# Query, key and value projections of an attention block as seven block products each, with the element-wise work spread anew over three engines

## The chip, the cores and the metric

The kernel runs on one core of a Trainium2 chip. A core has a matrix engine (TensorE, PE in the profile, with its weight loads as PEld), a vector engine (VectorE, DVE), a scalar engine (ScalarE, ACT), a general engine (GpSimd, POOL), and a queue that only issues transfers (SyncE, SP). Each engine takes its instructions in the order in which they were written, and waits for other engines by semaphores. Matrix products land in PSUM[...]; everything else lies in SBUF.

The metric is the time of one execution on the device in microseconds. Before the change it is 1538.98 us, the median of three runs (1535.9 to 1542.12).

## What is computed

Input x has 8 sequences of 1024 rows with 512 features. Cut to what matters, the reference is:

```python
def attention(x):                       # 16 heads of 32
    Q, K, V = split(x @ Wq.T + bq), split(x @ Wk.T + bk), split(x @ Wv.T + bv)
    scores = Q @ K.T / sqrt(32)
    scores = where(j > i, -inf, scores) - (i - j)     # causal, with linear decay
    return merge(softmax(scores) @ V) @ Wo.T + bo

def ffn(x):
    xh = x @ H                           # Hadamard matrix 512 x 512
    scale = max(abs(xh)) / 7             # per row
    xq = clip(round(xh / scale), -8, 7) * scale
    return xq @ ternary(weight).T

x = x + layernorm(attention(layernorm(x)))
x = x + layernorm(ffn(layernorm(x)))
```

## The kernel before

**Tiles.** Rows are worked on in 16 chunks of 512 (two to a sequence), each of four row tiles of 128. Features lie in four blocks of 128. Because of the decay, a query only needs keys of its own block of 128 rows and of the block before: `band()` computes that, and at its end a flag says whether the scores were small enough for this to be exact; otherwise `general()` is run as well. With the given inputs it is not.

**Per chunk.** `norm_in` loads a row tile (xc), normalises it (xn) and transposes it on TensorE into xnT, 128 features by 512 rows for each of four feature blocks. `project_k`, `project_q` and `project_v` (lines 149 to 165) each make one block of 128 x 512 of k, q or v: four matrix products of 128 x 128 by 128 x 512 that add up in one PSUM bank (`project`, line 146), emptied by ScalarE (lines 152, 157, 165). There are 12 such blocks a chunk. GpSimd squares k and q (line 294); from the squares a bound of the scores is made (`bound`, `shift`), which is the bias of the exponentials.

**Per unit.** A chunk has eight units, each four heads by half of the chunk's rows. `scores` does the products s (line 401) and four exponentials on ScalarE (line 414); `mask` cuts off the triangle on GpSimd (line 425); `add_keys` adds the two key blocks' exponentials into `both` on VectorE (line 439), for the sums of the softmax; `values` does the products with v and the sums (lines 454, 463); `divide` ends the unit on VectorE (lines 479 to 484).

**Per row tile.** `rest` is a generator whose `yield`s part it into steps: load xr (177); output projection o (146); y with its statistics (182); x1, and two levels of the Hadamard transform as sums and differences u and w, and the statistics of x1 (189 to 200); transposes of w, copied as wT (205, 207); h, the remaining transform by a 128 x 128 matrix (211); a correction of h's first column, maximum, scale, the rounding by adding a large number (qf, qi: 213 to 229); transposes of qi, copied as qiT (234, 236); f, the ternary product (146); y2 with statistics (241); the last sums and the store (248 to 250).

**What sets the order.** Nothing is scheduled automatically inside `band()`: each engine's queue follows the order of the calls. The main loop (lines 573 to 628) walks the units in pairs u = 0, 2, 4, 6. In a pair it mixes the scores of two units, the values of two, three projection blocks of the next chunk, one step sequence `norm` of the chunk after that, and the steps of two row tiles, `rest_b` (the older) and `rest_a`. The order in one pair, on TensorE, is: scores, values of the unit before, a projection block, transposes of qi, o, f, scores, a projection block, values, transposes of w, transposes of xn, a projection block, h. All PSUM results other than s and the values share one pool of three banks, so a result's bank is needed again three results later.

**Start and end.** Weights are loaded by transfers that ScalarE issues (`load_weights`), x by SP. The first chunk's projections run ahead of the main loop (lines 528 to 546), with the norms of the second chunk and the preparation of the ternary weight (`prepare`) among them. After the loop the last two row tiles run in step (lines 635 to 640).

## Time and profile before

| | |
|---|---|
| median of three runs | 1538.98 us (1535.9 to 1542.12) |
| the profiled execution | 1541.74 us, of which 1540.0 us from the first to the last instruction (the span) |
| mean granted clock of TensorE over the span | 0.976 of full speed |
| instructions | 26488 |
| projections of k, q, v on TensorE (512 product instructions each) | 239.8, 237.2 and 233.7 us of busy time |
| key sums on VectorE, `both` (128 instructions) | 156.9 us |
| mask on GpSimd (128) | 141.7 us |
| squares of k and q on GpSimd (64 each) | 81.9 and 73.2 us |
| exponentials on ScalarE (512) | 296.1 us |
| read from and written to HBM | 39.13 MB and 16.78 MB |

The page names a group of instructions by its line in the kernel, the engine, the operation, and the tiles written and read, then gives the number of instructions, their busy time in us and the mean of one in ns, and last the idle time of the engine just before them with what ended it. The chain of waits follows the program back from its last instruction, each time to what released it. The timeline lists instructions in the order of time; neighbours of one kind are merged. An answer by windows gives each engine's busy time in a stretch. Busy times of TensorE are modelled at their ends and overlap, so a chain's step is a better measure of what a group costs than the sum of its busy times.

### The profile page before, as it was taken

To read this page: it belongs to the slowest core of one execution; us is meant where nothing else is said; L and a number is where in the kernel's file an instruction comes from. 1 tells how busy PE (TensorE), PEld (TensorE's weight loads), DVE (VectorE), ACT (ScalarE), POOL (GpSimd) and SP (SyncE) were. 2 spreads that over 40 slices of the span, in tenths; PEclk is the share of its full clock that TensorE was granted. 3 is DMA by queue.
4 is the path that set the end of the run, shared out by engine and by line. 5 is a ranking of instruction groups with operands and counts; after the bars stand their busy time and mean duration, and the time that the engine had idled before them with its cause. 6 is when DMAs were issued, how large, how long until landed. Compare 5 with 4: busy or idle time off the path is not lost.

```text
span 1540.0 us, 26488 instructions
## 1 busy us (share of the span) xinstructions
PE 1467.9 (95%) x10428; PEld 774.2 (50%) x10428; DVE 1037.0 (67%) x2284; ACT 572.0 (37%) x961; POOL 755.8 (49%) x1118
## 2 busy tenths in 40 slices
PE   3799999999999999999999999999999999999884
PEld 2345555555555555555555555555555555554552
DVE  2145767776777767777777767776777767666685
ACT  1123434334433434343434334343433444343331
POOL 1223555545555464555545555554654555354443
PEclk9899999999999999999999999999999999999777
DMA  5010011011101101110111011011101110000010
GB/s 193 20 29 15 22 42 42 21 42 42 43 21 42 42 25 39 42 42 21 42 42 38 26 42 43 28 35 42 42 22 42 42 42 21 29 28 28 16 42 23
DMA packets 31766, 57.70 MB, mean 37 GB/s; under 512 B 4241, under 2 KB 4369, under 8 KB 31633
## 3 DMA queue, kind: packets, MB, share of 16 engines
q1 hardware_dynamic: 27648, 50.34, 9.7%
q10 hardware_dynamic: 3984, 5.58, 1.0%
q8 instruction: 84, 1.38, 0.4%
q14 instruction: 50, 0.40, 0.1%
HBM read 39.13 MB, written 16.78 MB: 36 GB/s over the span
## 4 chain that ended last, share of the span: by engine, by line
PE 93%; DVE 3%; POOL 1%; DMA 1%; ACT 1%; issue 1%; ACTq 0%; POOLq 0%; DVEq 0%
PE q_ps L146 15%; PE k_ps L146 15%; PE o_ps L146 15%; PE v_ps L146 15%; PE s L401 8%; PE av L454 8%; PE h_ps L211 4%; PE av L463 4%; PE f_ps L146 3%; PE wT_ps L205 2%; PE xnT_ps L138 2%; PE qiT_ps L234 1%; DMA wk_sb<-in_wkT 0%; PE m_ps L367 0%; DMA wv_sb<-in_wvT 0%
## 5 line engine op out<-in xcount | busy, mean ns | idle before, releaser
L414 ACT ACTIVATE pr<-s,bias 128x512 f32<-128x512 f32 (+1 forms) x512 | 296.1, 661 | 391.2 <-PE s L401 328.7
L425 POOL TENSOR_SCALAR_AFFINE_SELECT pr<-pr 128x1024 f32<-128x1024 f32 x128 | 141.7, 1107 | 253.9 <-ACT pr L414 253.7
L146 PE MATMUL k_ps<-xnT,wk_sb 128*128 128x512 f32 x512 | 239.8, 613 | 0.7 <-ACT xnT L526 0.7
L146 PE MATMUL q_ps<-xnT,wq_sb 128*128 128x512 f32 x512 | 237.2, 607 | 0.0
L146 PE MATMUL o_ps<-wo_sb,oT 128*128 128x512 f32 x512 | 234.5, 601 | 0.2
L146 PE MATMUL v_ps<-wv_sb,xnT 128*128 128x512 f32 x512 | 233.7, 600 | 0.1
L439 DVE TENSOR_TENSOR both<-pr 128x1024 f32<-128x1024 f32 (+1 forms) x128 | 156.9, 1226 | 49.6 <-POOL pr L425 25.0
L146 PEld LDWEIGHTS k_ps<-xnT,wk_sb 128*128 128x128 f32 x512 | 94.4, 194 | 110.8 <-issue 107.2
L146 PEld LDWEIGHTS q_ps<-xnT,wq_sb 128*128 128x128 f32 x512 | 93.3, 192 | 106.4 <-issue 104.2
L401 PE MATMUL s<-qT,kT 32*128 32x128 f32 (+1 forms) x2816 | 144.9, 333 | 0.0
L146 PEld LDWEIGHTS v_ps<-wv_sb,xnT 128*128 128x128 f32 x512 | 93.1, 192 | 99.8 <-issue 99.0
L146 PEld LDWEIGHTS o_ps<-wo_sb,oT 128*128 128x128 f32 x512 | 92.8, 191 | 95.5 <-issue 92.4
L115 POOL TENSOR_SCALAR rstd_a<-mv_a 128x1 f32<-128x1 f32 x64 | 14.3, 223 | 252.9 <-DVE mv_a L123 252.9
L401 PEld LDWEIGHTS s<-qT,kT 32*128 32x128 f32 x2816 | 116.9, 190 | 41.3 <-issue 31.3
L454 PE MATMUL av<-pr,v 128*32 128x128 f32 (+1 forms) x2816 | 134.9, 323 | 0.6 <-DVE h_ps L213 0.6
L294 POOL TENSOR_TENSOR sqk<-kT 128x512 bf16<-128x512 f32 x64 | 81.9, 1280 | 70.4 <-ACT kT L152 70.4
L454 PEld LDWEIGHTS av<-pr,v 128*32 128x32 f32 x2816 | 76.5, 112 | 78.1 <-POOL rstd_c L116 20.5
L182 DVE TENSOR_TENSOR y<-o_ps,bo 128x512 f32<-128x512 f32 x64 | 44.3, 692 | 93.9 <-PE o_ps L146 93.9
L152 ACT ACTIVATE kT<-k_ps,bk_sb 128x512 f32<-128x512 f32 x64 | 44.0, 688 | 160.7 <-PE k_ps L146 160.7
L134 DVE TENSOR_SCALAR xn<-xc,mv_n,rstd_n 128x512 f32<-128x512 f32 x60 | 32.8, 547 | 105.0 <-POOL rstd_n L116 105.0
L165 ACT COPY v<-v_ps 128x512 f32<-128x512 f32 x64 | 37.5, 586 | 160.0 <-PE v_ps L146 160.0
L213 DVE SCALAR_TENSOR_TENSOR h_ps<-mv_b,h_ps 128x1 f32<-128x1 f32 x64 | 10.5, 164 | 126.5 <-PE h_ps L211 126.5
(121 smaller groups left out, 2156.6 us busy)
## 6 DMA issues: line engine op xcount, KB each, us to landing
xr<-in_x SPq DMA_DIRECT2D x64, 256.0 KB, 3.0
out<-y SPq DMA_DIRECT2D x64, 256.0 KB, 2.0
xc<-in_x SPq DMA_DIRECT2D x60, 256.0 KB, 2.8
wk_sb<-in_wkT ACTq DMA_DIRECT2D x4, 256.0 KB, 5.7
x<-in_x SPq DMA_DIRECT2D x4, 256.0 KB, 5.4
wq_sb<-in_wqT ACTq DMA_DIRECT2D x4, 256.0 KB, 4.4
wf_sb<-in_wf ACTq DMA_DIRECT2D x4, 256.0 KB, 4.7
wv_sb<-in_wvT ACTq DMA_DIRECT2D x4, 256.0 KB, 5.3
```

The lines of the kernel that those rows point to most:

```text
L146: nc.tensor.matmul(ps, lhs(k), rhs(k), start=(k == 0), stop=(k == KD - 1))
L152: nc.scalar.activation(kT[:, o, :], ps, AF.Identity, bias=bk_sb[:, o : o + 1])
L165: nc.scalar.copy(v[:, t, :], ps)
L182: nc.vector.tensor_tensor(y, ps, bo2, ALU.add)
L211: nc.tensor.matmul(xh[:, k * P : (k + 1) * P], wT[:, k, :], had_sb, start=True, stop=True)
L294: nc.gpsimd.tensor_tensor(sq, src[:, o, :], src[:, o, :], ALU.mult)
L401: nc.tensor.matmul(s[:, hh, sc : sc + w], kc.kT[hsl, g, at * P : (at + 1) * P], ch.qT[hsl, g, q0 + qc : q0 + qc + w], start=True, stop=True,)
L414: nc.scalar.activation(pr[:, :, r0:, own, cols], s5[:, :, r0:, own, cols], AF.Exp, bias=ch.bias[:, own, h : h + 1],)
L425: nc.gpsimd.affine_select(out=own, in_=own, compare_op=ALU.is_ge, fill=0.0, base=0, pattern=[[0, HPG], [0, 2], [1, P]], channel_multiplier=-1,
L439: nc.vector.tensor_tensor(self.both[:, :, r0:], pr[:, :, r0:, 0, :], pr[:, :, r0:, 1, :], ALU.add)
L454: nc.tensor.matmul(av[hh * HD : (hh + 1) * HD, 0, qc : qc + w], kc.v[:, at, h * HD : (h + 1) * HD], pr[:, hh, sc : sc + w], start=(at_part ...
L463: nc.tensor.matmul(av[hh * HD : (hh + 1) * HD, 1, :], ones[:, :HD], self.both[:, hh].rearrange("p r c -> p (r c)"), start=True, stop=True, ...
```

## The change

**Seven products.** From the second chunk on, each of q, k and v is seen as a product of two matrices of 2 x 2 blocks, 256 wide, and made from seven block products in place of eight, after a scheme of sums and differences. The weights' combinations are made once (`Weight.combine`: three new tiles and two overwritten), those of x once per chunk on GpSimd (`Projections.combine`, four differences of 128 x 512). `product` does one block product: four matrix products with 256 columns (each runs as two passes), into one PSUM bank. What was one ScalarE copy per block becomes: product 1 is copied by ScalarE with the bias; the results of 2, 6, 7, 5, 4 and 3 are added on VectorE to a running sum or into the destination, product 5 twice. A pair of units takes five products (six in u = 6) instead of three blocks: two after the first scores, one after the second, two or three after the transposes of xn. The order of q and k is swapped.

**Other work moved.** xn: from VectorE to ScalarE, with a new GpSimd instruction for its bias (nmr). Key sums: from VectorE to GpSimd; the copy of the first units to ScalarE. Squares of k and q: from GpSimd to ScalarE, two instructions of 128 x 1024. The variance after h: no statistics of x1 and no correction of the first column any more; a Hadamard block with a zero first column (had0_sb), ScalarE's square with a sum (var), two GpSimd instructions. qf: from VectorE to ScalarE, in a step of its own, so that `rest` has 12 steps.

**Start and end.** wk and two biases are loaded by ScalarE's queue; wq, wf, wv, wo and the rest by SP's, behind the loads of x and xc, of which xc now has two buffers instead of three. The scale of q is put into wq by four ScalarE instructions. The norms of the second chunk are begun one projection ahead of their transposes. The last tiles are advanced by a written string of steps. Many row buffers go from two to one, k and v from three to two, for the room that the combinations take.

```diff
@@ norm_in @@
-        xn = pools.row.tile([P, D], F32, tag="xn", name=f"xn_{name}", bufs=2)
-        nc.vector.tensor_scalar(xn, xc, mv[:, 0:1], r, ALU.subtract, ALU.mult)
+        xn = pools.row.tile([P, D], F32, tag="xn", name=f"xn_{name}", bufs=1)
+        nmr = pools.small.tile([P, 1], F32, tag="nmr", name=f"nmr_{name}")
+        nc.gpsimd.tensor_scalar(nmr, mv[:, 0:1], r, -1.0, ALU.mult, ALU.mult)
+        nc.scalar.activation(xn, xc, AF.Identity, bias=nmr, scale=r)
@@ rest @@
-        mvb = stats(small, x1, f"b_{n}")
-        rb = rstd_of(small, mvb[:, 1:2], 1, f"rstd_b_{n}")
         yield
...
-        nc.vector.scalar_tensor_tensor(
-            xh[:, 0:1], mvb[:, 0:1], -math.sqrt(D), xh[:, 0:1], ALU.mult, ALU.add
-        )
+        nc.scalar.activation(sq, xh, AF.Square, accum_out=var)
+        rb = small.tile([P, 1], F32, tag="rstd1", name=f"rstd_b_{n}")
+        nc.gpsimd.tensor_scalar(rb, var, 1.0 / D, EPS, ALU.mult, ALU.add)
+        nc.gpsimd.tensor_tensor(rb, rb, neghalf[:, :1], ALU.pow)
+        yield
...
-        nc.vector.tensor_scalar(qf, xh, isc, ROUND, ALU.mult, ALU.add)
+        yield
+        nc.scalar.activation(qf, xh, AF.Identity, bias=round_col, scale=isc)
@@ squares @@
-            nc.gpsimd.tensor_tensor(sq, src[:, o, :], src[:, o, :], ALU.mult)
+            for o in range(0, KD, 2):
+                nc.scalar.activation(sq[:, o : o + 2, :], src[:, o : o + 2, :], AF.Square)
@@ Projections @@
+            ORDER = (1, 2, 6, 7, 5, 4, 3)
+            def combine(self, which):
+                if which == 0:
+                    nc.gpsimd.tensor_tensor(t[:, 0], b12, b11, ALU.subtract)
+                    nc.gpsimd.tensor_tensor(t[:, 1], b22, t[:, 0], ALU.subtract)
+                else:
+                    nc.gpsimd.tensor_tensor(t[:, 2], b22, b12, ALU.subtract)
+                    nc.gpsimd.tensor_tensor(t[:, 3], t[:, 1], b21, ALU.subtract)
+            def product(self):
+                for o in range(HB):
+                    osl = slice(o * P, (o + 1) * P)
+                    for i in range(HB):
+                        a, b = (x, w) if kind == 2 else (w, x)
+                        nc.tensor.matmul(
+                            ps[:, o, :], a[:, i, osl], b[:, i, :], start=(i == 0), stop=(i == HB - 1)
+                        )
...
+                elif which == 2:
+                    nc.vector.tensor_tensor(c11, ps, self.u, ALU.add)
+                elif which == 6:
+                    nc.vector.tensor_tensor(self.u, ps, self.u, ALU.add)
...
+                elif which == 5:
+                    nc.vector.tensor_tensor(c22, ps, self.u3, ALU.add)
+                    nc.vector.tensor_tensor(self.u, ps, self.u, ALU.add)
+                elif which == 4:
+                    nc.vector.tensor_tensor(c21, ps, self.u3, ALU.add)
+                else:
+                    nc.vector.tensor_tensor(c12, ps, self.u, ALU.add)
@@ Unit.add_keys @@
-                nc.vector.tensor_tensor(
+                nc.gpsimd.tensor_tensor(
                     self.both[:, :, r0:], pr[:, :, r0:, 0, :], pr[:, :, r0:, 1, :], ALU.add
                 )
@@ main loop, one pair @@
                 new.scores()
+                if proj and u == 0:
+                    proj.combine(0)
                 if unit:
                     unit.values()
                     unit.divide()
                 unit = new
+                steps(rest_a, 1)
                 unit.mask()
+                unit.add_keys()
+                if proj and u == 0:
+                    proj.combine(1)
+                products(proj, 1)
                 norm = next(norms_due)
                 steps(norm, 1)
-                unit.add_keys()
-                if proj:
-                    proj.project()
-                    proj.square()
+                products(proj, 1)
                 rest_b = rest_a
                 steps(rest_b, 1)
                 rest_a = next(rests_due) if at or u >= 4 else None
                 steps(rest_a, 1)
...
                 new = Unit(ch, before, u + 1)
                 new.scores()
-                    proj.project()
+                products(proj, 1)
                 steps(rest_b, 1)
                 new.mask()
                 steps(rest_a, 1)
-                if proj:
+                if proj and u == 2:
                     proj.square()
                 unit.values()
                 new.add_keys()
                 unit.divide()
                 unit = new
                 steps(rest_b, 1)
                 steps(rest_a, 1)
                 steps(norm, 1)
-                if proj:
-                    proj.project()
-                    proj.square()
-                steps(rest_a, 2)
+                products(proj, 1)
+                if proj and u == 2:
+                    proj.bound()
+                products(proj, 2 if u == 6 else 1)
+                steps(rest_a, 1)
+                if proj and u == 4:
+                    proj.square()
+                steps(rest_a, 1)
@@ after the loop @@
-        steps(rest_a, 1)
-        last = [next(rests_due), next(rests_due)]
-        for step in range(1, REST):
-            if step in (2, 3, 4):
-                steps(rest_a, 1)
-            for r in last:
-                next(r)
+        tails = {"r": rest_a, "a": next(rests_due), "b": next(rests_due)}
+        for which in "rrarbarabraabaabbabababbabb":
+            next(tails[which])
@@ load_weights @@
-        wq_sb = load_weight(wqT, "wq_sb")
+        wq_sb = load_weight(wqT, "wq_sb", nc.sync, wts)
-        wf_sb = load_weight(wf, "wf_sb", big, "pr")
-        wv_sb = load_weight(wvT, "wv_sb")
+        wf_sb = load_weight(wf, "wf_sb", nc.sync, big, "pr")
+        wv_sb = load_weight(wvT, "wv_sb", nc.sync, wts)
+    def prepare_q(wq_sb, bias=True):
+        for k in range(KD):
+            nc.scalar.mul(wq_sb[:, k, :], wq_sb[:, k, :], 1.0 / ROOT_HD)
```

## The prediction

> **What bounds the kernel now.** I read the page's engine shares and its chain first, then the chain and the timeline of one pair of units in mid-kernel, then the waits of TensorE and the last chunk, which has no projections.

> ```profile
> PE 1467.9 (95%) x10428; PEld 774.2 (50%) x10428; DVE 1037.0 (67%) x2284; ACT 572.0 (37%) x961; POOL 755.8 (49%) x1118
> PE 93%; DVE 3%; POOL 1%; DMA 1%; ACT 1%; issue 1%; ACTq 0%; POOLq 0%; DVEq 0%
> ```

> TensorE is busy 95% and is 93% of the chain. In the windows of 100 us that I took between 190 and 1390 it is busy 99.98 us of each: in mid-kernel it waits for nobody, so time falls only if its own work falls, and rises as soon as it must wait. One pair of units, from the chain (start, us, what):

> ```profile
> 709.27 0.89 PE h_ps L211 x8
> 710.16 1.09 PE s L401 x24
> 711.25 1.00 PE av L454 x24
> 712.25 0.43 PE av L463 x8
> 712.68 3.63 PE k_ps L146 x8
> 716.32 0.22 PE qiT_ps L234 x4
> 716.54 3.49 PE o_ps L146 x8
> 720.03 0.86 PE f_ps L146 x4
> 720.89 1.09 PE s L401 x24
> 721.98 3.63 PE k_ps L146 x8
> 725.61 1.01 PE av L454 x24
> 726.62 0.43 PE av L463 x8
> 727.05 0.59 PE wT_ps L205 x4
> 727.64 0.44 PE xnT_ps L138 x4
> 728.07 3.44 PE k_ps L146 x8
> 731.51 0.89 PE h_ps L211 x8
> ```

> A pair takes 732.40 - 710.16 = 22.24 us and holds three projection blocks. The reader is to see how much TensorE work lies ahead of each point where it needs another engine. The tightest is wT, which needs VectorE's w:

> ```profile
> 720.07 0.69 DVE L182 TENSOR_TENSOR y<-o_ps,bo 128x512 f32<-128x512 f32 x1 [1.85 <-PE o_ps L146]
> 721.62 0.73 DVE L241 SCALAR_TENSOR_TENSOR y<-f_ps,sc,wscale_row 128x512 f32<-128x512 f32 x1
> 725.11 0.42 DVE L198 TENSOR_TENSOR w<-u 128x256 f32<-128x256 f32 x1
> ```

> VectorE runs without a gap from the end of o (720.03) to the end of w (725.53): 5.5 us, of which y2 (L241), its statistics, x1, u and w are 3.91. TensorE comes to wT at 727.05: 1.5 us to spare. In the last chunk, without projections, the spare is gone:

> ```profile
> 1441.14 0.79 PE L205 MATMUL wT_ps<-ident,w 128*128 128x128 f32 x4 [1.93 <-DVE w L197]
> ```

> ```profile
> 1426.00:1432.00 6.00, 5.91 (x63) 4.01 (x63) 0.78 (x3) 2.42 (x4) 0.50 (x1) 0.50 0.01 3
> ```

> The second fence is a window of the last chunk (busy PE, PEld, DVE, ACT, POOL, then the granted clock): after TensorE stood 3.36 us (from 1422.7 to 1426.1) its clock is 0.50 for six microseconds.

> [...] of five idle times of 3.36 to 3.42 us (34.0, 47.7, 65.4, 72.9, 1422.7) four were followed by 0.50, for about 6.7 us each time it can be timed. [...] here the add L249 takes 1263 ns for 512, so I estimate 2.4 us for 1024. [...] here rstd_b's pow took 1.54 us beside the add at L439 and 0.57 for rstd_n.

> **The change part by part**, on one chunk of four pairs (u = 0, 2, 4, 6).

> TensorE's own work. A pass of 512 columns takes 3.44/8 = 430 ns, one of 128 columns (h) 0.89/8 = 111; on the line between, 256 columns cost 217. Twelve blocks of 3.44 = 41.3 us become 21 of 8 x 217 ns = 36.5: -4.8 per chunk, -72 over 15 chunks (the first keeps whole products). Weight loads (190 ns mean) still fit under 217; if they did not, +0.5 per chunk. TensorE's floor is then 20.6 us a pair, plus one product of 1.73 in u = 6.

> The sums on VectorE: seven of about 0.69 and one more for "5", 14 us a chunk, against 20 removed (8 key sums of 1.28, st_b, xn, qf, the fix of h). Its load falls, so by share nothing is lost. What counts is place. VectorE takes its queue in order, and in the changed order the queue reads: y (o), its statistics, the sum of the pair's third product, y2 (f), statistics, x1, u, w. On TensorE: o, f, scores, third product, values (1.44), wT. So the sum cannot begin before the third product ends, and w follows it by 0.69 + 0.04 + 3.91 = 4.65, with about 0.1 to hand over. TensorE has only the values to do meanwhile: it waits 4.75 - 1.44 = 3.3 us at wT. Before, ScalarE emptied that block and y2 did not wait. This holds in u = 0 (product 6 of q), u = 4 (4 of k) and u = 6 (7 of v); in u = 2 the third product is 1 of k, emptied by ScalarE, and only the shorter spare bites: 5.5 + 0.1 against 0.86 + 1.09 + 1.92 + 1.44 = 5.3, so 0.3. Behind the waiting sum stand all of y2, x1, u, w, the division and the next sums; wT on TensorE waits for them, and all of TensorE behind wT.

> The GpSimd queue. Key sums 2.4 each, +19 less what the short units save, combinations of x 4 x 1.26 = 5, squares of 1.21 x 8 gone: some 16 us a pair of 24, not its bound. But place again: xn now is ScalarE's and waits for nmr, which waits behind mask and key sum on GpSimd, and qiT's copy stands behind xn on ScalarE. From the end of h: exps end 3.65, mask 4.8, key sum 7.2, rstd and nmr 8.3, xn 9.2, copy 9.8; f is reached at 9.9. It just fits. In u = 0 the four combinations stand in that queue (two before mask, two before rstd; net 3.0): f waits 3.0, about 2.3 in chunks whose first units have half a key sum.

> ScalarE. Squares of k (two of about 1.1) stand between h's Square and the exps of u = 6: qf and qi come late, 0.75 at qiT and 0.8 more at f. In u = 2 the squares of q delay wT's copy, whose PSUM buffer the next product but one needs: 0.9 to 1.1. Elsewhere the new Square, qf, xn (about 0.7 to 0.8 each) lie beside TensorE's work: qi is ready at 4.9, wanted at 6.2.

> Sum of waits: u = 0 6.3, u = 2 1.4, u = 4 3.3, u = 6 4.85: 15.85, or 14.95 in the other kind of chunk; 15.4 x 13, 12.7 for the chunk without norms, 6.5 for the first, where most rests are missing: +219.

> The clock. Waits of about 3.0 to 3.3: 43 at wT, some 10 at f. Not quite the 3.36 of the trace, so I take six in ten to halve the clock, at 3.0 us lost each (half of 6.7, less what falls into the wait): +95. From below 0 [...], from above all of them, +160.

> Start. Before, ScalarE issues the loads until 20.45 and k starts at 24.2; then four waits of 3.4 for xn behind GpSimd's squares (34.0, 47.7, 65.4, 72.9), with a halved clock after most. After, ScalarE issues wk and two biases alone, xn's chain stands a block ahead of its transposes, the squares go to ScalarE. New: the third xc load waits for a buffer freed by xn of the first tile, and wq, wf, wv, wo queue behind it on SP, so wq lands about 30; its scaling holds ScalarE till 32, and q needs it about 34. Scores begin near 74 instead of 99: -25; bounds -10 and -30.

> End. In the last chunk qi now passes exps and a second engine, +1.5 a pair; the staggered last tiles, one key sum of 2.4 for one of 1.28, -3 in all: +3, bounds -8 and +12. Other moves (st_b, fix of h, both's copy) lie under TensorE either way.

> Total against the profiled 1540.0: 1540 - 72 + 219 + 95 - 25 + 3 = 1760. That run took 1541.74 with what lies around the span, 2.8 above the median of the three runs: 1757.

> **Rivals.**
> - The waits come, the clock stays: 1757 - 95 = 1662. For: no wait of 3.3 stands alone in this trace. Against: four of five at 3.4.
> - Half the waits are taken up elsewhere (a buffer or a sum that I placed too late), little clock: 1540 - 72 + 110 - 25 = 1553, up to 1600.
> - Faster: the waits at wT stay under 1.6 us. Place: VectorE's queue between y and w, where the sum would have to be done by the time that f's result comes. At three per chunk that is the 4.8 saved; below it the fewer products decide, and with no waits the time is 1540 - 72 - 25 - 3 = 1440. For: TensorE is 93% of the chain and every other engine has a third of its time free. Against: the third product ends 3 us after f, and no queue is overtaken.
> - The products are not fewer: excluded by the changed order, 21 blocks of 256 columns a chunk.

> **How the numbers follow.** Forecast 0.66, clock stays 0.16, half the waits 0.07, faster 0.11. The range 1630 to 1820 leaves out the faster case, the half case and a tail of the clock's upper bound. A change under 0.5% can't be told from none; hardly any case ends there: faster 0.10, same 0.01, slower 0.89.

> **What would show it.** In the changed profile: TensorE busy under 90%, wT waiting for w about 45 times by about 3.3 us, f for the copy of qiT once a chunk; granted clock near 0.9; chunks of about 107 us instead of 90; passes of 256 columns at 217 ns; scores starting before 80. A wT wait near zero, or chunks under 90 us, would prove me wrong.

## The result, and the profile after

The changed kernel takes 1753.11 us (median of four runs, 1751.9 to 1754.21), the kernel before 1538.56 us in the four runs made with it: 1.1393 times as long, with a 95% interval of 1.1367 to 1.1418. The forecast was 1757. The profiled execution took 1754.21 us, with a span of 1752.5.

Of the page of the changed kernel, the engine shares, the chain by engine, and two groups of instructions:

```profile
PE 1488.5 (85%) x11508; PEld 1024.8 (58%) x11508; DVE 978.3 (56%) x2159; ACT 698.6 (40%) x1208; POOL 925.3 (53%) x1252
...
PE 47%; POOL 20%; DVE 14%; issue 10%; ACT 8%; DMA 1%; POOLq 0%; SPq 0%; ACTq 0%; DVEq 0%
...
L543 POOL TENSOR_TENSOR both<-pr 128x1024 f32<-128x1024 f32 (+1 forms) x128 | 269.7, 2107 | 10.7
...
L203 PE MATMUL wT_ps<-ident,w 128*128 128x128 f32 x256 | 60.8, 336 | 143.4 <-DVE w L197 143.1
```

TensorE was 93% of the chain and is now 47% of it. No engine took its place by load: VectorE's share fell from 67% to 56%, and GpSimd is busy for 53%. The chain passes from engine to engine. The waits of TensorE (who waited, for whom, then the sum in us, how often, the longest) name the places:

```profile
PE wT_ps L203 <- DVE w L197: 143.1, 57, 4.3
PE f_ps L152 <- ACT qiT L244: 37.0, 35, 3.1
PE qiT_ps L242 <- DVE qi L237: 21.1, 21, 5.1
```

Before, wT waited 13.9 us in six times, and f had no entry. One stop for each of the two first lines, from TensorE's timeline of a pair with u = 0 (start, duration, line, tiles, count, and in brackets the idle time just before and who ended it):

```profile
798.97 1.04 PE L152 MATMUL f_ps<-ternT,qiT 128*128 128x512 bf16 x4 [3.10 <-ACT qiT L244]
799.93 1.16 PE L505 MATMUL s<-qT,kT 32*128 32x256 f32 x24
801.02 1.99 PE L373 MATMUL q_ps<-T,wq_s 128*128 128x256 f32 x8
802.95 1.08 PE L558 MATMUL av<-pr,v 128*32 128x256 f32 x24
803.84 0.61 PE L567 MATMUL av<-both,ones 128*32 128x256 f32 x8
807.30 0.92 PE L203 MATMUL wT_ps<-ident,w 128*128 128x128 f32 x4 [2.85 <-DVE w L197]
808.02 1.05 PE L144 MATMUL xnT_ps<-ident,xn 128*128 128x128 f32 x4
808.87 3.16 PE L373 MATMUL q_ps<-T,wq_sb 128*128 128x256 f32 x8
811.87 1.89 PE L373 MATMUL q_ps<-T,wq_s 128*128 128x256 f32 x8
```

Some 5.5 us of work lie between the two stops. After the second, the four transposes of xn take 1.05 us where 0.60 is usual, and the next product 3.16 where the one after it takes 1.89: the granted clock is 0.50 from 808.02 to 811.43.

The other side of a stop at wT is in VectorE's timeline, here of a pair with u = 4, where k's sum (L418) is the third product's:

```profile
847.96 0.18 DVE L127 BATCH_NORM_AGGREGATE mv_a<-st_a 128x2 f32<-128x6 f32 x1
850.70 0.69 DVE L418 TENSOR_TENSOR kT<-k_ps,u_k 128x512 f32<-128x512 f32 x1 [2.55 <-PE k_ps L373]
851.30 0.74 DVE L249 SCALAR_TENSOR_TENSOR y<-f_ps,sc,wscale_row 128x512 f32<-128x512 f32 x1
...
854.46 0.42 DVE L197 TENSOR_TENSOR w<-u 128x256 f32<-128x256 f32 x1
```

First VectorE stands 2.55 us, since the sum at the head of its queue waits for TensorE's product. The result of f (TensorE's f began at 846.61) lies ready behind it. Then y2, the statistics, x1, u and w run, and TensorE stands: its wT began at 854.94, after 2.85 us of idle time. Two engines wait for each other in turn, and neither is full.

Divided by stages, from the two traces:

| stage | before, us | after, us | difference | forecast |
|---|---|---|---|---|
| start, to the first scores of the first unit | 99.2 | 72.0 | -27.2 | -25 |
| loop, as long as projections run (15 chunks) | 1323.5 | 1542.3 | +218.8 | +242 |
| last chunk and last tiles | 117.3 | 138.2 | +20.9 | +3 |
| sum | 1540.0 | 1752.5 | +212.5 | +220 |

### The profile page after: what moved, and what is told of

Read it like the earlier page. It is cut to its first block, busy times and chain, and to the rows that moved or that the text cites. A ratio compares the mean times of both kernels' runs of the same rounds, so it can differ in the third digit from the quotient of the medians.

```text
span 1752.5 us, 29131 instructions
## 1 busy us (share of the span) xinstructions
PE 1488.5 (85%) x11508; PEld 1024.8 (58%) x11508; DVE 978.3 (56%) x2159; ACT 698.6 (40%) x1208; POOL 925.3 (53%) x1252
## 3 DMA queue, kind: packets, MB, share of 16 engines
q10 hardware_dynamic: 864, 1.05, 0.2%
## 4 chain that ended last, share of the span: by engine, by line
PE 47%; POOL 20%; DVE 14%; issue 10%; ACT 8%; DMA 1%; POOLq 0%; SPq 0%; ACTq 0%; DVEq 0%
PE v_ps L373 8%; PE q_ps L373 8%; POOL both L543 6%; PE k_ps L373 6%; PE s L505 4%; POOL pr L529 4%; PE o_ps L152 4%; PE h_ps L209 3%; PE f_ps L152 3%; PE wT_ps L203 3%; DVE st_c L126 2%; DVE y L249 2%; DVE x L189 2%; PE xnT_ps L144 2%; ACT xh L218 2%
## 5 line engine op out<-in xcount | busy, mean ns | idle before, releaser
L543 POOL TENSOR_TENSOR both<-pr 128x1024 f32<-128x1024 f32 (+1 forms) x128 | 269.7, 2107 | 10.7
L203 PE MATMUL wT_ps<-ident,w 128*128 128x128 f32 x256 | 60.8, 336 | 143.4 <-DVE w L197 143.1
L140 ACT ACTIVATE xn<-xc,nmr,rstd_n 128x512 f32<-128x512 f32 x60 | 48.8, 813 | 244.7 <-POOL nmr L139 244.7
L256 ACT ACTIVATE y<-y,cc,rstd_c 128x512 f32<-128x512 f32 x64 | 52.2, 816 | 183.7 <-POOL cc L254 179.2
L218 ACT ACTIVATE xh<-h_ps 128x512 bf16<-128x512 f32 x64 | 38.3, 598 | 216.2 <-PE h_ps L209 216.2
L182 DVE TENSOR_TENSOR y<-o_ps,bo 128x512 f32<-128x512 f32 x64 | 44.1, 689 | 143.4 <-PE o_ps L152 143.4
L119 POOL TENSOR_SCALAR rstd_c<-mv_c 128x1 f32<-128x1 f32 x64 | 39.5, 617 | 155.0 <-DVE mv_c L127 155.0
L152 PE MATMUL f_ps<-ternT,qiT 128*128 128x512 bf16 x256 | 68.8, 393 | 38.9 <-ACT qiT L244 37.0
L228 DVE TENSOR_REDUCE sc<-h_ps 128x1 f32<-128x512 f32 x64 | 44.2, 691 | 86.3 <-ACT xh L218 86.3
L257 POOL TENSOR_TENSOR y<-y,x 128x512 f32<-128x512 f32 x64 | 81.7, 1276 | 3.1 <-ACT y L256 1.8
L567 PE MATMUL av<-both,ones 128*32 128x256 f32 x1024 | 78.7, 379 | 0.0
```

The source lines that it names most:

```text
L119: nc.gpsimd.tensor_scalar(r, var, EPS, None, ALU.add)
L152: nc.tensor.matmul(ps, lhs(k), rhs(k), start=(k == 0), stop=(k == KD - 1))
L203: nc.tensor.transpose(pt[:, k, :], w[:, k // 2, k % 2, :], ident)
L218: nc.scalar.activation(sq, xh, AF.Square, accum_out=var)
L257: nc.gpsimd.tensor_tensor(y2, y2, x1, ALU.add)
L543: nc.gpsimd.tensor_tensor(self.both[:, :, r0:], pr[:, :, r0:, 0, :], pr[:, :, r0:, 1, :], ALU.add)
```

## The experiments

Two theories were set against each other. The first is the forecast's: the time is lost by place, as VectorE's and GpSimd's queues hold early work behind late work. The second: it is lost by amount, as engines now have more to do beside each other (sums from PSUM, key sums on GpSimd, more loads of weights). Each ratio is to the kernel before, in runs on the same chip.

| kernel | median, us | ratio (95% interval) | clock of the profiled run |
|---|---|---|---|
| after, with the third product's sum late | 1590.43 | 1.034 (1.0314 to 1.0365) | 0.972 |
| the same, copy of qiT ahead of xn | 1549.83 | 1.007 (1.0045 to 1.0094) | 0.975 |
| the same, reordered further | 1519.12 | 0.9875 (0.9847 to 0.9903) | 0.975 |
| the same, qi early at the end | 1498.24 | 0.9726 (0.9713 to 0.9739) | 0.981 |
| after, stops at wT filled with products | 1693.34 | 1.1003 (1.0977 to 1.1029) | 0.976 |
| before, one block in three emptied by VectorE | 1811.52 | 1.1763 (1.174 to 1.1787) | 0.932 |
| before, key sums on GpSimd | 1538.77 | 0.9997 (0.9982 to 1.0012) | 0.976 |
| after, qi early at the end | 1736.49 | 1.1292 (1.1259 to 1.1326) | 0.947 |
| after, last key sums on VectorE | 1752.42 | 1.1393 (1.1365 to 1.142) | 0.938 |
| after, both of these | 1739.05 | 1.1307 (1.1274 to 1.134) | 0.942 |
| after, loads on ScalarE's queue | 1754.27 | 1.139 (1.1368 to 1.1412) | 0.94 |
| reordered, more moves in mid-kernel | 1524.42 | 0.9902 (0.9883 to 0.9921) | 0.976 |

### The third product's sum behind w

One instruction group is moved: in u = 0, 4 and 6 the third product's sum goes behind w in VectorE's queue. Nothing is taken away.

```diff
-                products(proj, 1)
+                if proj:
+                    proj.product(late=u != 2)
                 steps(rest_b, 1)
                 new.mask()
                 steps(rest_a, 1)
+                if proj and u != 2:
+                    proj.gather(*proj.late)
```

> The third product's sum is put behind w in VectorE's queue, in u = 0, 4 and 6; nothing else changes. Theory 1 (y2, x1, u and w stood behind a sum that waits for the third product): the wT waits fall from 143 us to about 25 (0.3 each in mid-kernel, the last chunk's stay), and with 43 long stops gone most of the clock's loss goes too: 1753 - 118 - 75 = about 1560, granted clock over 0.97. Theory 2 (VectorE is just late after o, whatever stands in its queue, or GpSimd's key sums take over as the next limit): wT still waits 2 us or more on average and the time stays above 1680.

1590.43 us: 162.7 less than the changed kernel, from the place of one sum in a queue. Its waits of TensorE:

```profile
PE f_ps L152 <- ACT qiT L244: 37.0, 35, 3.1
PE wT_ps L203 <- DVE w L197: 31.8, 30, 3.4
PE qiT_ps L242 <- DVE qi L237: 24.1, 21, 5.1
```

The wait at wT falls by 111 us, and the others stay as they were, to a few us. So 111 of the 162.7 are the wait itself; the clock, 0.972 against 0.938, has most of the rest. It is 30 us above the number of the first theory and 90 below that of the second.

### The same stops, filled with work

The clock's part alone: where TensorE stands at wT, the sums of the softmax are computed six times over instead of once, so that nothing arrives earlier or later but TensorE is busy meanwhile.

```diff
-                for hh in range(HPG):
-                    nc.tensor.matmul(
...
+                for _ in range(repeat):
+                    for hh in range(HPG):
+                        nc.tensor.matmul(
...
-                unit.values()
+                unit.values(6 if proj and u != 2 and rest_a else 1)
```

> The changed kernel with the eight sum products of the values (0.43 us) issued six times instead of once where the wait at wT follows, so that TensorE works 2.15 us of the 3.3 that it would stand; the results are the same. Theory 1 (the stops halve the granted clock, and that costs as much again as two thirds of the waits): the waits at wT shrink by 2.15 each because they are filled, nothing waits longer, the granted clock rises from 0.938 to 0.97 or more, and the time falls by about 70 us to 1680. Theory 2 (the clock is no part of it; the low clock is that of the last chunk and the start): the time stays at 1750 or rises by some us.

1693.34 us, 59.8 less than the changed kernel although TensorE does more. A window of 100 us (start and end, length, then busy PE, PEld, DVE, ACT and POOL with their counts, granted clock, DMA share, GB/s), first of the changed kernel, then with the fill:

```profile
800.00:900.00 100.00, 89.17 (x739) 64.04 (x739) 58.42 (x129) 41.60 (x72) 55.58 (x71) 0.95 0.10 33
```

```profile
800.00:900.00 100.00, 93.53 (x847) 64.64 (x850) 60.38 (x134) 44.29 (x81) 56.68 (x78) 1.00 0.10 33
```

The wait at wT falls by 97 us (143.1 to 46.2). The fill takes five times 0.43 us (the group of eight passes, as the trace of before has it) at 44 stops, 95 us. These two cancel, to 2 us; what remains, some 60 us, is the clock after these stops. The record of the clock agrees: TensorE was at half clock for 219 us in the changed kernel and for 83 with the fill, and half of the difference is 68. The forecast had put 95 on these stops and on ten at f.

### The mechanism without the change

If a late sum in VectorE's queue is the cause, it must do the same in the kernel before, with eight products and no key sums on GpSimd. There, one projection block in each pair, the one between the second scores and the values, is emptied by VectorE instead of ScalarE.

```diff
+        if dve:
+            nc.vector.tensor_copy(v[:, t, :], ps)
+            return
         nc.scalar.copy(v[:, t, :], ps)
...
-                    proj.project()
+                    proj.project(dve=True)
```

> The kernel before, whole products and all, with one change: the middle projection block of each pair is emptied by VectorE instead of ScalarE (one instruction of about 0.69 us, so 41 us more of VectorE's 1037). Theory 1 (an emptying that waits for a late product, ahead of y2, x1, u and w in VectorE's queue, stops TensorE at wT, whatever the products are): about 57 waits at wT of 3.3 us = 190, and by what the filled waits showed (60 us of clock for 43 waits) some 75 of clock: about 1800. Theory 2 (the waits belong to the seven products, the short blocks or the moved work): VectorE has a third of its time free, and the time stays within 1535 to 1560.

1811.52 us. VectorE got 60 instructions of 0.69 to 0.75 us more, 44 us of work on an engine with a third of its time free, and the kernel lost some 272 us. TensorE's wait, and VectorE's timeline around one copy:

```profile
PE wT_ps L216 <- DVE w L208: 185.1, 64, 4.4
```

```profile
819.30 0.69 DVE L174 COPY v<-v_ps 128x512 f32<-128x512 f32 x1 [3.14 <-PE v_ps L146]
819.91 0.74 DVE L252 SCALAR_TENSOR_TENSOR y<-f_ps,sc,wscale_row 128x512 f32<-128x512 f32 x1
```

The copy waits 3.14 us at the head of the queue, with y2 behind it, as in the changed kernel. The seven products are not needed for the loss: an emptying at this place in VectorE's queue is enough.

### Key sums on GpSimd, alone

```diff
-                nc.vector.tensor_tensor(
+                nc.gpsimd.tensor_tensor(
                     self.both[:, :, r0:], pr[:, :, r0:, 0, :], pr[:, :, r0:, 1, :], ALU.add
```

> The kernel before with the key sums on GpSimd and nothing else. Theory 1 (moving work to GpSimd costs nothing while its sum is not behind a product and nothing of the next tile waits behind it): between 1535 and 1550. Theory 2 (a key sum of 2.4 us on GpSimd, after the mask, makes the values late by itself): TensorE waits at the values, over 1560.

1538.77 us, the same as before to 0.2%. The move that adds most work to GpSimd costs nothing in the kernel before. Of what the second theory names, this takes out the key sums; the sums from PSUM and the loads of weights are all still there in the reordered kernels below, and the last of those are faster than the kernel before.

### The copy of qiT ahead of xn

To the late sum one move is added: the second tile's norm, with nmr on GpSimd and xn on ScalarE, is issued after the transposes of qi and their copy. In the kernel with the late sum alone, the chain of waits showed why f was late (start, us, what), here in a chunk whose first units have half a key sum:

```profile
806.43 1.30 POOL pr L537
...
807.81 1.27 POOL both L551
809.08 1.23 POOL T L356
810.30 1.22 POOL T L357
...
812.60 0.28 POOL nmr L139
...
812.90 0.81 ACT xn L140
813.72 0.48 ACT qiT L244
...
814.24 0.39 PE f_ps L152
```

Mask, key sum, two differences of x and three small instructions on GpSimd, then xn, then the copy of qiT: f hangs on a chain of which it needs only the last step.

```diff
                 norm = next(norms_due)
-                steps(norm, 1)
                 products(proj, 1)
                 rest_b = rest_a
                 steps(rest_b, 1)
+                steps(norm, 1)
```

> As e1, and xn's chain (statistics, rstd, nmr, xn) is issued after qiT's transposes and copy, so that the copy no longer stands behind xn on ScalarE. Theory 1 (f waits because the copy stands behind xn, which waits for GpSimd): the 37 us of waits at f go to under 5, a few of the clock's drops with them: 45 to 55 us less than e1, about 1510. Theory 2 (f waits because ScalarE itself is late with the exponentials, Square and qf): 10 us less than e1 or nothing.

1549.83 us, 40.6 less than without the move, a little under the 45 to 55 expected. The wait of f for qiT's copy, 37.0 us, is down to 1.6.

### Further moves

Three more late things are taken from ahead of early ones: a pair's first product goes ahead of mask and key sum; the squares and the bounds go behind the copy of qiT and behind o (at u = 4 and 6); the copy of wT goes ahead of the older tile's last step.

```diff
                 steps(rest_a, 1)
+                products(proj, 1)
                 unit.mask()
...
-                products(proj, 1)
                 norm = next(norms_due)
...
+                if proj and u in (4, 6):
+                    proj.square()
                 steps(norm, 1)
...
-                steps(rest_b, 1)
                 steps(rest_a, 1)
+                steps(rest_b, 1)
                 steps(norm, 1)
```

> As e3, with four more changes of order: the pair's first product ahead of mask and key sum; the squares of q and k behind qiT's copy in u = 4 and 6, their bounds behind o; wT's copy ahead of the last step of the older tile on ScalarE. Theory 1 (what is left of the loss in mid-kernel is such waits on ScalarE's queue, about 1.5 to 2.5 us in each of u = 0, 2 and 6): a chunk falls from 90 to 87 us or less and the time by 30 to 45 us, to about 1512. Theory 2 (mid-kernel is at its floor and the rest is the end): 1540 or more.

1519.12 us, 7 above the number expected, and faster than the kernel before by 1.25%. In mid-kernel (200 to 1300 us) one kind of wait is left, that of wT for w, 23.1 us in 38 times, 0.6 us each, and the granted clock is 1.00 from 600 to 1300 us. The same instructions that cost 14% more than before are now cheaper than before.

An attempt to take the remaining waits as well (y2's statistics in a step of their own behind w, and one bound later) missed:

```diff
+        yield
...
-        for which in "rrarbarabraabaabbabababbabb":
+        for which in "rrarbarrabraabaabbababaabbabbb":
```

> As e4, with the last chunk's qf and qi ahead of its scores (as t2), y2's statistics behind w in a step of their own, and the bound of q behind y. Theory 1 (what e4 has left is 0.7 us at each wT, since y2's statistics stand ahead of w, and the end): waits at wT in mid-kernel under 8 us instead of 29, the end 15 us shorter: 1475 to 1485. Theory 2 (the next limit is as near): over 1495.

1524.42 us, 5.3 more than without these moves, although it also had the earlier qi at the end that is described below. Its waits between 200 and 1300 us:

```profile
PE k_ps L374 <- ACT wT L205: 11.4, 6, 1.9
PE q_ps L374 <- ACT wT L205: 7.0, 6, 1.2
...
PE wT_ps L203 <- DVE w L197: 4.6, 13, 0.5
```

The wait at wT fell from 23.1 to 4.6 us, and came back as products that wait for a PSUM bank: the copy of wT is late, and so is the bank that it empties. Which of the moves did that was not taken apart.

### The end

The end was 18 us longer than forecast. Three variants of the changed kernel were made for it: the key sums of the last chunk back on VectorE; qf and qi of the last chunk, which has no projections, ahead of the pair's scores; and both.

```diff
+                if not proj:
+                    steps(rest_a, 1)
                 new = Unit(ch, before, u)
                 new.scores()
...
-                steps(rest_a, 1)
+                if proj:
+                    steps(rest_a, 1)
                 unit.mask()
```

Last key sums on VectorE:

> The changed kernel with the key sums of the last chunk alone back on VectorE. The end took 20.9 us more than before where I had forecast 3. Theory 1 (in the last chunk values wait for GpSimd's key sum, the division for the values, qi for the division): about 10 us less, 1743. Theory 2 (qi is late because qf now waits behind the exponentials on ScalarE): 0 to 2 us less.

1752.42 us: no gain where 10 us were expected. On VectorE the key sum stands ahead of the division and waits for the mask (1.41 us, for the one that starts at 1653.41).

The step with qi early:

> The changed kernel where, in the last chunk alone, qf and qi are issued ahead of the scores, so that qf stands before the exponentials on ScalarE and qi before the division on VectorE. Theory 1 (the end is long because qi waits behind a division that waits for the values): 8 to 12 us less than 1753. Theory 2 (it is long because the key sum on GpSimd takes 2.4 us): the values wait as before, 3 us less at most.

1736.49 us, 16.6 less than the changed kernel and more than the 8 to 12 expected. TensorE's transposes of qi in three successive pairs of the last chunk, first of the changed kernel, then with qi early:

```profile
1644.02 0.40 PE L242 MATMUL qiT_ps<-ident_bf,qi 128*128 128x128 bf16 x4 [2.17 <-DVE qi L237]
1665.54 0.61 PE L242 MATMUL qiT_ps<-ident_bf,qi 128*128 128x128 bf16 x4 [5.06 <-DVE qi L237]
1688.00 0.40 PE L242 MATMUL qiT_ps<-ident_bf,qi 128*128 128x128 bf16 x4 [2.09 <-DVE qi L237]
```

```profile
1635.77 0.40 PE L242 MATMUL qiT_ps<-ident_bf,qi 128*128 128x128 bf16 x4 [2.67 <-DVE qi L237]
1653.20 0.40 PE L242 MATMUL qiT_ps<-ident_bf,qi 128*128 128x128 bf16 x4 [2.67 <-DVE qi L237]
1670.63 0.40 PE L242 MATMUL qiT_ps<-ident_bf,qi 128*128 128x128 bf16 x4 [1.10 <-DVE qi L237]
```

The reader is to look at the distances: 21.5 and 22.5 us a pair against 17.4 and 17.4. The waits in brackets changed less than the distance. The chain of waits says why: in the changed kernel qi, once ready, stands in VectorE's queue behind the division, which waits for the pair's last products.

```profile
1641.42 0.49 PE av L567 x8
1641.93 0.46 DVE sumT L583
...
1643.13 0.42 DVE oT L588
1643.55 0.42 DVE qi L237
1644.02 0.40 PE qiT_ps L242 x4
```

So all of scores, values and division lie on the chain of the row tile, once a pair. With qi early they run beside it.

Both edits together:

> As t2 with the last chunk's key sums on VectorE too. If both stand in the path: 4 us or more below t2. If the key sum doesn't matter: as t2 within 2 us.

1739.05 us, 2.6 more than with qi early alone: moving the key sum back gains nothing here either.

### The reordered kernel with qi early

The edit of the end, on top of the further moves:

> The order of e4 with one edit more: in the last chunk, which has no projections, the step with qf and qi stands ahead of the pair's first scores, as in t2. Theory 1 (the end's loss is qi behind the division, whatever the rest of the order is): the gain of t2, 16.6 us, comes again, as the end of e4 is as long as that of the changed kernel (140.7 us from the flag's products to the end, against 138.2) and TensorE waits there 19.9 us for qi: 1519.1 - 14 to 17, about 1503 to 1505, a ratio near 0.977; TensorE's wait for qi falls under 5 us. Rival (the wait goes to another place of the same chain, as in e5): 1510 to 1519, with waits of TensorE for the copy of qiT or of wT in the last chunk in its place.

1498.24 us (1496.6 to 1498.87, five runs), 20.9 less, where 14 to 17 were expected, and 0.9726 of the kernel before (0.9713 to 0.9739). The loop ends at the same place (the flag's products begin at 1377.15, against 1376.6): all of the gain is at the end, 120.0 us from there against 140.7. (The 138.2 of the expectation is counted from the end of the loop; from the flag's products the changed kernel takes 135.4.) The wait for qi is 7.9 us, not under 5. Engine shares and waits of this kernel:

```profile
PE 1400.8 (94%) x11508; PEld 972.2 (65%) x11508; DVE 974.6 (65%) x2159; ACT 706.3 (47%) x1208; POOL 924.5 (62%) x1252
```

```profile
PE wT_ps L203 <- DVE w L197: 42.2, 50, 4.0
...
PE qiT_ps L242 <- DVE qi L237: 7.9, 4, 4.1
```

The instruction counts are those of the changed kernel's page (11508, 2159, 1208 and 1252). It does the same work in another order and is 254.9 us faster.

### The loads

All weights are issued by ScalarE again, the rest of the start left as changed.

```diff
-        wq_sb = load_weight(wqT, "wq_sb", nc.sync, wts)
+        wq_sb = load_weight(wqT, "wq_sb", nc.scalar, wts)
...
-            nc.sync.dma_start(wo_sb[:, k, :], woT[k * P : (k + 1) * P, :])
+            nc.scalar.dma_start(wo_sb[:, k, :], woT[k * P : (k + 1) * P, :])
```

> The changed kernel with all weights loaded by ScalarE's queue again, as before. Theory 1 (the 27 us gained at the start are for the larger part the four waits for xn behind GpSimd's squares, and their clock; the queue of the loads is worth the earlier first product, 19.8 against 24.2): 4 to 8 us more than 1753. Theory 2 (the queue of the loads is what gained): 15 us more or above.

1754.27 us: no difference that can be told from none, and the first scores begin at 74.96 instead of 72.02. Of the 27.2 us gained at the start, some 3 are the loads' queue. The other 24 stay when the loads go back. The four waits for xn of 3.4 us each that stood ahead of the first scores are gone in both kernels; which of the other moves took them away was not tested.

## Why the prediction was right

The mechanism was right: VectorE's queue, with a sum that waits for its product ahead of work that is ready, stops TensorE at wT, and f waits for a copy behind xn. So were its signs: TensorE is busy for 85%, the granted clock is 0.938, a chunk takes 103 us (forecast 107), and the first scores begin at 72. That the time came so close, 1753 against 1757, is in part luck: the loop grew by 23 us less than forecast and the end by 18 more, and within the loop waits and clock were 49 us less than forecast, while 26 us came that no term has.

- **The wait at wT.** Forecast: 43 waits of 3.3 us, as the third product's sum stands ahead of y2 in VectorE's queue. In the loop's trace 44 waits are longer than 1.5 us, and 41 of these are 2.85 or 3.07 long. The kernels with the late sum and with the copy on VectorE show the cause from both sides. The 0.4 us too much is a detail of the step: I let wT wait for both halves of w; its idle time ends with the first (L197), and the second half, 0.42 us, then holds up the second of the four transposes.
- **The other waits.** The loop's waits were to be 219 us in sum; the trace has 190 between 72 and 1614 us: wT 131.6, f 35.3, o 5.7 and 3.0, nq 5.0, qiT 4.8, xnT 3.2, and entries of 1 us and less. The mis-sized terms are those for the squares on ScalarE. The squares take 1.05 and 1.07 us each, as worked out, but the "0.75 at qiT" came out as 0.3 at most, and the "0.9 to 1.1" at the bank of wT as 0.5 at most: the copies had more time to spare than I had counted. The key sum on GpSimd, estimated at 2.4 us, takes 2.38 (mean of the 96 of 128 x 1024). At f, the 0.8 of u = 6 came out as 0.25. In u = 0, f waited what its term says in the chunks with whole key sums, 3.10 us in the fence above for 3.0; in the others it waited 1.38, for 2.3, after 0.81 at o.
- **The clock.** "Six in ten to halve the clock, at 3.0 us lost each": both factors were estimates, from five idle times of the trace before, and both were wrong. Of the 44 stops at wT, 37 (more than eight in ten) were followed by a halved clock, and of the seven stops of 3.1 us at f only one. The price was lower: of the 39 halved stretches in the loop, 34 last 3.41 us and five last 6.83, where I had taken 6.7 for all from what follows the longer idle times of the kernel before (there, too, the one after 72.9 lasts only 3.41). That makes 150 us at half clock, and 75 lost. From another side: the filled stops gave back 60 us, about 1.4 a stop. The term was +95.
- **The rest of the loop.** -72, +190 and +75 make +193, and the loop grew by 219. The 26 us between them are not the products': counted from each start to the next instruction's, idle time left out, those of the loop took 636.5 us before and take 565.4 in the fastest kernel, whose granted clock is 1.00 in five windows of 100 us taken between 200 and 1200, so TensorE's own gain is 71, as forecast. Some 12 us are the stops' own. After its wait, the group of wT takes 0.72 us until the next group starts (807.30 to 808.02 above), against 0.49 before, as the second transpose waits for the second half of w: 0.23 us in each of 51 waits. The other 14 have no name here.
- **Start.** -25 against -27.2. Which part of it is due to what was not all as said: the loads' order, to which the working gives half its words, is worth about 3.
- **End.** The step that failed: "In the last chunk qi now passes exps and a second engine, +1.5 a pair". From one group of qi's transposes to the next, the last chunk's pairs took 20.1, 21.5, 22.5 and 19.7 us, against 18.1, 17.4, 17.2 and 16.4 before: 2.0 to 5.2 more. I had counted the instructions that qi passes, and not that on VectorE it now stands behind a division that waits for TensorE. It is the argument of the wait at wT, applied to the loop and left out for the end. With qi early, the part from the flag's products on is 119.7 us, against 113.9 before and 135.4 in the changed kernel; that is +5.8, near the forecast's +3.
- **The rival on the faster side** named the right place and price: VectorE's queue between y and w. With that sum moved and two more queues put in order, the kernel is faster than before: 1519 and 1498 against 1539. Not all of that is due to the fewer products. In the profiled run of the fastest kernel, the start is 27 us shorter and the loop 21, and the end is 5 longer; the 71 us saved by the products pay for what else the loop still loses. No run has the new order with whole products.
- **A slip in the working.** Of the sums on VectorE it counts seven, and one more for product 5; there are six and one more for each of q, k and v, as product 1 goes to ScalarE. The 14 us a chunk are right.

## What to carry to other kernels

When an engine's output is given to another engine to empty, ask not how full that engine is but what will stand behind the new instruction in its queue, and how long the instruction will wait at the head for its input. Here one sum of 0.69 us, issued before its product was done and ahead of work that was ready, cost 163 us; the same sum put behind that work cost nothing that could be seen. A saving of TensorE's work shows only once every such place is in order: look for the pair of idle times, on one engine waiting for a product and shortly after on TensorE waiting for that engine, and go on after the loop, where less work covers the same chain.

## What was unexpected of the hardware

```profile
746.58:749.99 3.41, 1.88 (x35) 0.90 (x33) 2.86 (x5) 1.07 (x2) 0.55 (x1) 1.00 0.00 0
749.99:753.41 3.42, 2.09 (x13) 1.80 (x14) 2.97 (x9) 1.46 (x3) 3.07 (x6) 1.00 0.00 0
...
804.61:808.02 3.41, 0.71 (x4) 0.52 (x5) 3.27 (x9) 0.08 (x1) 2.32 (x5) 1.00 0.01 2
808.02:811.43 3.41, 3.41 (x13) 2.84 (x11) 1.03 (x3) 1.70 (x3) 3.33 (x3) 0.50 0.00 0
```

The first stop is divided between two windows, and TensorE is busy for more than half of each; the clock stays. The second lies almost whole in one window, busy for 0.71 us, and the next window runs at half clock. Counted from 100 to 1560 us of the changed kernel: 37 windows at full clock were followed by a halved one, and TensorE was busy for 2 to 45% of them; of the 349 that were not, none was under 42% and only seven under 47%. In the kernel before with the copy on VectorE it is, over the same stretch, 48 windows of at most 46% against 331 of 51% or more. So in these two traces every window at full clock that was busy for less than 42% was followed by one at half clock, and none that was busy for more than 47% was. The window of the second stop was busy for 21%; none of the 37 was idle throughout.

**An instruction of 0.43 us that took 2.27.** In the kernel before, each of the 64 instructions that write qi takes 0.426 to 0.429 us. In the changed kernel (VectorE's group for qi: shortest, median and longest in ns, first and last start) they don't:

```profile
L237 DVE TENSOR_SCALAR qi<-qf x64: 416/751/2268, 136.9 to 1733.6; 128x512 bf16<-128x512 f32 x64
```

The longest ran from 1663.22 to 1665.49; GpSimd's key sum ran from 1662.86 to 1665.20. It is the stop of 5.06 us of the last chunk shown above. With the last key sums on VectorE, that wait is 2.07. It is not the only one: in 61 of the 64 cases a GpSimd instruction was under way when qi began (52 times the mask, seven times a difference of x, twice a key sum), and in 60 of these qi ended 0.28 us after that instruction. The 61st began 0.01 us after a key sum did and took 0.42 us; the three that met no GpSimd instruction took 0.42 or 0.43. In the kernel before, none of the 64 began beside one. What holds qi back, and why it is 0.28 us from the end of the other instruction to its own, and not 0.43, the traces don't show. It is one more reason to ask, of a key sum of 2.38 us that is moved to GpSimd, which short instruction of VectorE may meet it.
